# A gated expert layer on one core: the first pass's residual moved into the carried sums, and its results stored piece by piece

## The chip, the cores and the metric

The kernel runs on one core of one Trainium2 chip. The metric is the device time of one execution in microseconds (us), the median of several runs. The core has five engines that run side by side and meet at semaphores: PE (TensorE, matmuls; its weight loads are shown as PEld), DVE (VectorE), ACT (ScalarE), POOL (GpSimd) and SP (SyncE, which here issues nearly all DMAs).

## The reference

For eight batches of 512 rows and width 256, with nine "experts" (eight gated ones and a shared one) of inner width 1024:

```python
g = jnp.einsum('bsd,edf->ebsf', h, Wg)
u = jnp.einsum('bsd,edf->ebsf', h, Wu)
expert_outs = jnp.einsum('ebsf,efd->ebsd', jax.nn.silu(g) * u, Wd)
expert_output = jnp.einsum('be,ebsd->bsd', gating_probs, expert_outs)
shared = jnp.einsum('bsf,fd->bsd', jax.nn.silu(h @ Sg) * (h @ Su), Sd)
sg = shared_gate_prob[:, :, None]
return (1.0 - sg) * expert_output + sg * shared      # added to x
```

The result is `x` plus this. The `x +` is the residual that the change is about. All is in float32.

## The kernel before, in words

**Passes and units.** The eight batches are done in two passes (`h` = 0 and 1) of four. A pass goes through the nine experts, each in two groups of 512 inner columns, so it has 18 units and the kernel 36 (`u.n` = 0 to 35). A unit multiplies four blocks of weight columns (index i) with four batches (index j). To save products, blocks and batches are combined in pairs in the manner of fast matrix multiplication: `CI` holds the four numbers 0, 1, -1, 2, and `PAIRS` the six pairs.

**The hub basis.** Each batch is held transposed, in two halves of 128 features. `xhub[h, i][:, 1]` is the second half, X1. `xhub[h, i][:, 0]` is X0 - c X1, with c = `CI[i]`. Results come in the same basis: `acc["b", i]` is the first half of the result, `acc["B", i]` the second half plus c times the first; when a pass closes, c times the first is taken off.

**G steps and D steps.** `gate_up` makes the gate and up products of a unit in 52 G steps: 16 hub steps (`P_step`, `Q_step` and the first `R1_step`s), then six per pair (`R1_step`, two `R_step`s, twice). `down` makes the down products in 26 D steps: three for each pair, then `p0` to `p3` and `q0` to `q3`. PE does them in an order that is written out by hand, two G and one D in turn (`"GGD"`). The `down` of a unit starts at G step 22 of that unit and ends at G step 22 of the next one, so its eleven last steps (p0, q0, pair 5, q1, p1, q2, p2, q3, p3) lie in the first 11 D steps of the next unit.

**Carried banks.** D products go to two PSUM banks in turn (`po0`, `po1`). A "p" step is `carried`: ACT copies the running sum `acc["b", i]` into the bank (L578, the seed), PE adds its product (L579), ACT copies the bank back to SBUF (L587). A "q" step is `single`: PE writes the bank (L595) and DVE adds it to `acc["B", i]` (L566). The bank is free for the next product but one when that is done. The sums S of four pairs are carried like p.

**Who orders what.** Within `manual_schedule` the order on PE and POOL follows the program (and on ACT in unit 0). The order on DVE, SP, and on ACT from unit 1 on is laid out at build time by a planner that works with estimated durations. Each engine then runs its list in order, so an instruction that waits holds up all that stand behind it.

**Forms.** In unit 0 the pair forms of x are made on the chip: `x_difference` (DVE L288, ACT L290), `x_sums` (DVE L302 and POOL L303), `w_difference` (POOL L384) and `w_sums` (ACT L394, POOL L396 and L397). `store_forms` writes the x forms to DRAM. In later units SP loads them again: `v` by L292, `b` (two buffers) by L309. `prepare(1)` makes those of the second pass, in parts, during units 2 to 17. POOL also adds up the inner results for the p and q steps (`add_sum`, L540).

**The end of the first pass.** Unit 17 closes the pass; its last D steps lie in unit 18. `turn_back`, called at D steps 6, 10, 11, 13, 15, 18, 20 and 23 of unit 18, turns a result half with DVE (L669), adds x (L670), and after the second half of a batch stores four pieces of 128 KB (L673). x itself was loaded by `load_back` (L659) in four pieces per batch: two batches in unit 17, two more when buffers come free in unit 18. These tiles come from `iopool`, which has two buffers.

**The end of the second pass** has its own steps (`end_step`, `tail`, `store_rows`); its stores wait in a list, `end_stores`, of which one is issued per G step.

Of the kernel before, what the change touches and what calls it, by code (L numbers as in the profile page):

```python
# [16 lines left out]
def kernel(  # L17
# [95 lines left out]
    def make_coef():  # L113
# [4 lines left out]
            gp.tensor_tensor(coef[:, e, :], gt[:, :, e], rest, ALU.mult)  # L118
        gp.tensor_copy(coef[:, E, :], sgt)

    scratch = {}
    back = {}
    xhub = {}
    xdram = {}

# [424 lines left out]
    def down(u, acc):  # L550

        def tile_of(key):
            acc[key] = apool.tile(
                [P, S], F32, tag=f"acc{key[0]}{key[1]}", name=f"acc{key[0]}{key[1]}_{u.h}"
            )
            return acc[key]

        def put(key, bank, s):

            if key not in acc:  # L560
                if s == 1.0:
                    nc.scalar.copy(tile_of(key), bank)
                else:
                    nc.scalar.mul(tile_of(key), bank, s)
            elif s == 1.0:
                ve.tensor_add(acc[key], bank, acc[key])  # L566
            elif s == -1.0:
                ve.tensor_sub(acc[key], acc[key], bank)
            else:
                ve.scalar_tensor_tensor(acc[key], bank, s, acc[key], ALU.mult, ALU.add)  # L570

        def seeded(key, w, b):

            po, k = new_po(f"{key[0]}{key[1]}_{u.name}")
            full = key in acc and not turned[k]
            turned[k] = False
            if full:
                nc.scalar.copy(po, acc[key])  # L578
            nc.tensor.matmul(  # L579
                po, w, b, start=not full, stop=True, skip_group_check=full  # L580
            )
            return po, full

        def carried(key, w, b):
            po, full = seeded(key, w, b)
            if full:
                nc.scalar.copy(acc[key], po)  # L587
            else:
                put(key, po, 1.0)
            return po if full else acc[key]  # L590

        def single(key, w, b):
            po, k = new_po(f"{key[0]}{key[1]}_{u.name}")
            turned[k] = False
            nc.tensor.matmul(po, w, b, start=True, stop=True)  # L595
            return po, k

        def pair(p):
            i, j = PAIRS[p]
            d = CI[i] - CI[j]  # L600
            A, k = single(("r", p), u.Wd[p][i], u.h_[i, j])
            put(("B", j), A, 1.0)
            held[k] = True
            yield
            args = u.Wd[p][j], u.h_[j, i]
            if p in OWN and not closes(u):
                carried(("S", p), *args)
            else:
                if p in OWN:
                    o, full = seeded(("S", p), *args)  # L610
                    if not full:
                        ve.tensor_add(o, o, acc["S", p])
                else:
                    o, _ = single(("s", p), *args)
                put(("B", i), o, -1.0)
                put(("V", p), o, -1.0)
            yield
            nc.tensor.matmul(  # L618
                A, u.Ud[p], u.X[p], start=False, stop=True, skip_group_check=True
            )  # L620
            if closes(u):
                ve.tensor_add(A, A, acc["V", p])
                put(("b", i), A, 1.0 / d)
                put(("b", j), A, -1.0 / d)
            else:
                put(("V", p), A, 1.0)
            held[k] = False
            po_next[0] = 1 - k
            yield

        done = {}
        for what in (0, 1, 2, 3, 4, "p0", "q0", 5, "q1", "p1", "q2", "p2", "q3", "p3"):
            if isinstance(what, int):
                yield from pair(what)
                continue
            i = int(what[1])
            if what[0] == "p":
                flush_sums(u, "rows", i)
                done[what] = carried(("b", i), u.raw_d[:, i, 0:P], u.rows[i])
            else:  # L640
                flush_sums(u, "cols", i)
                po, _ = single(("q", i), u.ad[i], u.cols[i])
                put(("B", i), po, 1.0)
                done[what] = po
            if closes(u) and f"p{i}" in done and f"q{i}" in done:
                if CI[i] != 0.0:
                    put(("B", i), done[f"p{i}"], -CI[i])
                for r in (0, 1):
                    ends[u.h, i, r] = acc["bB"[r], i]
            yield  # L650

    BACK = [(0, 1), (0, 0), (2, 1), (2, 0), (1, 1), (1, 0), (3, 1), (3, 0)]

    def load_back(h, i):

        if (h, i) not in back:
            xr = iopool.tile([P, S // 32, 2, 32], F32, tag="io", name=f"xr{h}_{i}")
            for q in range(4):
                nc.sync.dma_start(xr[ts(q, 32)], squares(x, NI * h + i, q))  # L659
            back[h, i] = xr  # L660
        return back[h, i]

    def turn_back(h, i, r):

        b = NI * h + i
        block = ends.pop((h, i, r))
        xr = load_back(h, i)
        t = zpool.tile([P, S], F32, tag="z", name=f"to{b}_{r}")
        ve.transpose(t, block)  # L669
        ve.tensor_add(xr[:, :, r], t.rearrange("p (c d) -> p c d", d=32), xr[:, :, r])  # L670
        if (i, 1 - r) not in BACK[BACK.index((i, r)):]:
            for q in range(4):
                nc.sync.dma_start(squares(out, b, q), xr[ts(q, 32)])  # L673
            if i in (0, 2):
                load_back(h, i + 1)

    last_rows = {}
    tails = {}
    ended = {}
    end_rows = {}  # L680
    end_stores = []

    def end_step(kind, i):

        b = NI * (NH - 1) + i
        if kind == "turn":
            t = iopool.tile([P, 2, S], F32, tag="io", name=f"end{i}")
            for r in range(2):
                ve.transpose(t[:, r], ends.pop((NH - 1, i, r)))
            ended[i] = t  # L690
        elif kind == "store":
            to = end_rows[i] = dram.tile([S, D], F32, tag=f"end{i}", name=f"endrows{i}")
            at = to.rearrange("(c r t) d -> r t c d", r=32, t=NT)
            for r in range(2):
                for q in range(4):
                    end_stores.append((
                        at[:, :, :, ts(4 * r + q, 32)],
                        ended[i][ts(q, 32), r].rearrange("r (t c d) -> r t c d", t=NT, d=32),
                    ))
        elif kind == "x":  # L700
            last_rows[i] = load_rows(xpool, "x", b)
        elif kind == "load":
            at = end_rows[i].rearrange("(p t) d -> p t d", t=NT)
            end_rows[i] = []
            for c in range(2):
                t = sumpool.tile([P, 2, D], F32, tag="sum", name=f"endin{i}_{c}")
                nc.sync.dma_start(t, at[:, 2 * c : 2 * c + 2])
                end_rows[i].append(t)
        else:
            for xr, t in zip(last_rows[i], end_rows[i]):  # L710
                gp.tensor_tensor(xr, xr, t, ALU.add)
# [28 lines left out]
    def gate_up(u, nxt):  # L740
# [5 lines left out]
        def sums(p):  # L746
            x_sums(u, p)
            w_sums(u, p)
# [35 lines left out]
        for p in range(len(PAIRS)):  # L784
# [13 lines left out]
            for m in range(2):  # L798
                if not last:
                    R1_step(u, p + 1, m)  # L800
                    if m == 0 and u.n == 0 and p and p + 1 < len(PAIRS):
                        sums(p + 1)
                elif nxt is not None:
                    P_step(nxt, 0, m)
                yield
                for r in range(2):
                    R_step(u, p, m, r)
                    if m == 1 and r == 1:
                        h_sums(u, p)
                        if u.n == 0 and p + 2 < len(PAIRS):  # L810
                            seed(u, p + 2)
                        if p + 2 < len(PAIRS) and u.n:
                            sums(p + 2)
                    yield

# [16 lines left out]
        34: (("add", 1),), 37: (("load", 2),), 40: (("add", 2),), 44: (("load", 3),),  # L832
        47: (("add", 3),),
    }

    TAKE = 22

# [27 lines left out]
    for u in units:  # L865
# [6 lines left out]
        for what in FIRST if u.n == 0 else LAST if nxt is None else ORDER:  # L872
            if what == "G":
# [5 lines left out]
                    behind = down(u, acc) if nxt is not None else iter(())  # L879
                if final and nxt is not None and nG in (18, 21, 24, 27):  # L880
                    load_x(u.h + 1, (nG - 18) // 3)
                if final and nxt is not None and nG in (30, 36):
                    load_back(u.h, (nG - 30) // 3)
                if nxt is None:
                    for what_, i in END_STEPS.get(nG, ()):
                        end_step(what_, i)
                    if end_stores:
                        nc.sync.dma_start(*end_stores.pop(0))
                if nG > TAKE and nG % 2 == 0 and u.sums:
                    add_sum(u)  # L890
                for _ in range(2 if u.n and units[u.n - 1].opens else 1):
# [67 lines left out]
```

## Time and profile before

| what | us |
|---|---|
| median of 3 runs (lowest 2446.30, highest 2447.63) | 2446.37 |
| the profiled execution | 2446.47 |
| its span, first to last instruction | 2444.7 |
| PE busy in the span | 2431.5 |
| POOL busy | 2080.0 |
| DVE busy | 1928.9 |
| ACT busy | 1239.4 |

The granted clock of TensorE has a mean of 0.999. Lines of the profile name the engine, the line of the kernel (L513), the operation, and the tiles as out<-in. Lines of the timeline begin with the start and the length in us; "x2" means that two records were put together, and a bracket at the end tells how long the engine stood idle before and what released it. One float32 product of 128x128 by 128x512 is two records on PE. DMA issues are shown at the queue that issues them, SPq.

### The profile page before, as it was taken

The numbers are of one execution on the slowest core, as the hardware profiler recorded it, in microseconds if no ns is written. First come the engines' busy times: TensorE is split into PE (matmuls) and PEld (weight loads), VectorE is DVE, ScalarE is ACT, GpSimd is POOL, SyncE is SP. The second block draws the span as 40 slices with busy tenths as digits, with TensorE's granted clock in tenths as the row PEclk, the third lists the DMA queues.
The fourth block names the chain that finished last, engine by engine and source line by source line (L and its number), as shares of the span: only waits on it lengthen the run. The fifth ranks groups of instructions, "written<-read, shape, count | busy, mean of one in ns | idle before, by whom it ended". The sixth has DMA issues, their size and how long they took to land.

```text
span 2444.7 us, 22778 instructions
## 1 busy us (share of the span) xinstructions
PE 2431.5 (99%) x5736; PEld 1085.1 (44%) x5736; DVE 1928.9 (79%) x2870; ACT 1239.4 (51%) x2294; POOL 2080.0 (85%) x2313
## 2 busy tenths in 40 slices
PE   9999999999999999999999999999999999999999
PEld 4444444444444444444444444444444444444446
DVE  7778878777777877787987777777777777777795
ACT  5555554554555555555445555555555555555542
POOL 8988888898988989898878888888888888888872
PEclk9999999999999999999999999999999999999999
DMA  4333343343433333344353233323333333233245
GB/s 158 101 105 111 104 112 112 103 134 102 126 110 97 105 111 97 106 129 125 112 118 120 85 95 91 91 81 99 99 104 103 95 97 92 88 91 92 86 117 149
DMA packets 237841, 260.02 MB, mean 106 GB/s; under 512 B 80656, under 2 KB 173072, under 8 KB 237712
## 3 DMA queue, kind: packets, MB, share of 16 engines
q1 hardware_dynamic: 236880, 258.27, 35.9%
q8 instruction: 48, 0.79, 0.1%
q14 instruction: 81, 0.66, 0.1%
q10 hardware_dynamic: 832, 0.30, 0.0%
HBM read 240.69 MB, written 17.83 MB: 106 GB/s over the span
## 4 chain that ended last, share of the span: by engine, by line
PE 96%; POOL 1%; DVE 1%; DMA 1%; issue 0%; ACT 0%; SPq 0%; ACTq 0%; DVEq 0%; POOLq 0%
PE c L513 30%; PE c L503 15%; PE c L481 10%; PE c L458 10%; PE r L595 7%; PE r L618 7%; PE S L579 5%; PE b L579 5%; PE q L595 5%; PE s L595 2%; PE tail L720 1%; DMA sgt<-ondB_sharedgateprob_dram 0%; POOL wd L429 0%; POOL wb L396 0%; DVE h L449 0%
## 5 line engine op out<-in xcount | busy, mean ns | idle before, releaser
L513 PE MATMUL c<-b,wb 128*128 128x512 f32 x1728 | 848.1, 593 | 2.6 <-DMA b<-xs 1.9
L444 ACT ACTIVATE sg<-c 128x512 f32<-128x512 f32 x576 | 343.8, 597 | 595.0 <-DVE c L518 343.7
L449 DVE SCALAR_TENSOR_TENSOR h<-sg,coef,c 128x512 f32<-128x512 f32 x576 | 427.8, 743 | 235.6 <-PE c L513 128.3
L513 PEld LDWEIGHTS c<-b,wb 128*128 128x128 f32 x1728 | 328.3, 190 | 412.9 <-issue 390.0
L503 PE MATMUL c<-v,u 128*128 128x512 f32 x864 | 441.5, 593 | 1.9 <-ACT c L498 1.4
L540 POOL TENSOR_TENSOR rows<-rows,h 128x512 f32<-128x512 f32 x280 | 369.0, 1318 | 0.0
L508 DVE TENSOR_TENSOR c<-D,c 128x512 f32<-128x512 f32 x432 | 298.7, 692 | 81.1 <-ACT sg L444 61.4
L540 POOL TENSOR_TENSOR cols<-cols,h 128x512 f32<-128x512 f32 x280 | 357.7, 1277 | 0.0
L518 DVE TENSOR_TENSOR c<-c,D 128x512 f32<-128x512 f32 x432 | 298.6, 691 | 22.3 <-PE c L513 22.1
L396 POOL TENSOR_TENSOR wb<-u,wb 128x256 f32<-128x256 f32 x108 | 79.2, 733 | 237.3 <-ACT wb L394 237.3
L458 PE MATMUL c<-x,w 128*128 128x512 f32 x572 | 274.5, 592 | 0.0
L503 PEld LDWEIGHTS c<-v,u 128*128 128x128 f32 x864 | 163.0, 189 | 210.0 <-issue 163.9
L595 PE MATMUL r<-h,wd 128*128 128x512 f32 x420 | 215.4, 594 | 0.0
L618 PE MATMUL r<-X,ud 128*128 128x512 f32 x420 | 214.5, 592 | 0.0
L529 DVE TENSOR_TENSOR X<-h,h 128x512 f32<-128x512 f32 x210 | 206.1, 982 | 6.8
L481 PE MATMUL c<-x,at 128*128 128x512 f32 x432 | 209.4, 593 | 1.2 <-DVE P L474 0.7
L491 ACT COPY D<-c 128x512 f32<-128x512 f32 x284 | 165.8, 584 | 83.8 <-DVE h L449 83.8
L540 POOL TENSOR_TENSOR rows<-h,h 128x512 f32<-128x512 f32 x140 | 195.4, 1396 | 0.0
L540 POOL TENSOR_TENSOR cols<-h,h 128x512 f32<-128x512 f32 x140 | 181.0, 1293 | 0.0
L464 ACT COPY P<-c 128x512 f32<-128x512 f32 x216 | 126.6, 587 | 106.9 <-PE c L458 102.3
L458 PEld LDWEIGHTS c<-x,w 128*128 128x128 f32 x572 | 108.5, 190 | 135.9 <-issue 111.9
L578 ACT COPY S<-accS 128x512 f32<-128x512 f32 x132 | 77.9, 590 | 149.8 <-DVE accV L566 140.7
(108 smaller groups left out, 3472.5 us busy)
## 6 DMA issues: line engine op xcount, KB each, us to landing
b<-xs SPq DMA_DIRECT2D x210, 512.0 KB, 3.6
v<-xs SPq DMA_DIRECT2D x210, 256.0 KB, 2.6
wd<-in_L_cond_Wd_dram SPq DMA_DIRECT2D x32, 512.0 KB, 4.9
w<-in_L_cond_Wg_dram SPq DMA_DIRECT2D x127, 128.0 KB, 3.5
w<-in_L_cond_Wu_dram SPq DMA_DIRECT2D x127, 128.0 KB, 3.6
f<-xd SPq DMA_DIRECT2D x12, 512.0 KB, 3.6
xs<-f SPq DMA_DIRECT2D x18, 256.0 KB, 3.0
xin<-in_x_dram SPq DMA_DIRECT2D x16, 256.0 KB, 4.1
```

The lines of the kernel that those rows point to most:

```text
L444: nc.scalar.activation(s, bank, AF.Silu)
L449: ve.scalar_tensor_tensor(t, u.sg[i, j], coef[:, u.e, b : b + 1], bank, ALU.mult, ALU.mult)
L458: nc.tensor.matmul(bank, u.raw[i][:, m, 0], xhub[u.h, i][:, 0], start=True, stop=True)
L481: nc.tensor.matmul(bank, u.at[i][:, m], xhub[u.h, i][:, 1], start=False, stop=True, skip_group_check=True,)
L503: nc.tensor.matmul(bank, u.U[p][:, m], u.V[p], start=False, stop=True, skip_group_check=True)
L508: ve.tensor_sub(other, u.Ds[j, m], bank)
L513: nc.tensor.matmul(bank, u.W[p][:, r, m], u.VB[p][:, r], start=False, stop=True, skip_group_check=True,)
L518: ve.tensor_add(bank, bank, u.Ds[j, m])
L540: gp.tensor_tensor(sums[n], u.h_[n, n] if first else sums[n], u.h_[at], ALU.add)
L579: nc.tensor.matmul(po, w, b, start=not full, stop=True, skip_group_check=full)
L595: nc.tensor.matmul(po, w, b, start=True, stop=True)
L618: nc.tensor.matmul(A, u.Ud[p], u.X[p], start=False, stop=True, skip_group_check=True)
```

## The change

- The residual of the first pass is no longer loaded and added at the end. It is added in 14 of the units 3 to 16, one term in each: where a p or q step of that unit is due, its bank is seeded from the running sum and copied out by DVE with `acc = xhub * s + po` (`carried_with`). The terms per batch i are X0 - c X1 plus c times X1 for the b sum, and (1 + c c) X1 plus c (X0 - c X1) for the B sum; terms with factor 0 are left out. For q this puts a seed copy ahead of the product.
- `turn_back` only transposes, straight into the strided store tile; `load_back` and its calls are gone. The four store pieces of a batch go into a list, `outgoing`, of which one is issued per G step in any unit. The end of the second pass uses the same list.
- In unit 0, `sums(p + 2)` is called after the last `R_step` of pair p, as in the other units, and no longer after the `R1_step` that opens the next pair.
- A helper, `issue_after`, is defined and not called.

```diff
-            if what[0] == "p":
+            extra = carry_on.get(u.n)
+            if extra is not None and extra[0] == what:
+                flush_sums(u, "rows" if what[0] == "p" else "cols", i)
+                if what[0] == "p":
+                    key, w, b = ("b", i), u.raw_d[:, i, 0:P], u.rows[i]
+                else:
+                    key, w, b = ("B", i), u.ad[i], u.cols[i]
+                carried_with(key, w, b, *extra[1:])
+            elif what[0] == "p":
...
+        def carried_with(key, w, b, half, s):
+            po, full = seeded(key, w, b)
+            assert full
+            ve.scalar_tensor_tensor(
+                acc[key], xhub[u.h, key[1]][:, half], s, po, ALU.mult, ALU.add
+            )
...
+    for i in range(NI):
+        c = CI[i]
+        for what, half, s in (("p", 0, 1.0), ("q", 1, 1.0 + c * c), ("p", 1, c), ("q", 0, c)):
+            if s != 0.0:
+                carry_on[3 + len(carry_on)] = f"{what}{i}", half, s
...
     def turn_back(h, i, r):
 
-        b = NI * h + i
-        block = ends.pop((h, i, r))
-        xr = load_back(h, i)
-        t = zpool.tile([P, S], F32, tag="z", name=f"to{b}_{r}")
-        ve.transpose(t, block)
-        ve.tensor_add(xr[:, :, r], t.rearrange("p (c d) -> p c d", d=32), xr[:, :, r])
+        if i not in backs:
+            backs[i] = iopool.tile([P, S // 32, 2, 32], F32, tag="io", name=f"to{h}_{i}")
+        t = backs[i]
+        ve.transpose(t[:, :, r], ends.pop((h, i, r)).rearrange("p (c d) -> p c d", d=32))
         if (i, 1 - r) not in BACK[BACK.index((i, r)):]:
             for q in range(4):
-                nc.sync.dma_start(squares(out, b, q), xr[ts(q, 32)])
-            if i in (0, 2):
-                load_back(h, i + 1)
+                outgoing.append((squares(out, NI * h + i, q), t[ts(q, 32)]))
...
-                    if m == 0 and u.n == 0 and p and p + 1 < len(PAIRS):
-                        sums(p + 1)
...
-                        if p + 2 < len(PAIRS) and u.n:
+                        if p + 2 < len(PAIRS):
                             sums(p + 2)
...
-                if final and nxt is not None and nG in (30, 36):
-                    load_back(u.h, (nG - 30) // 3)
...
-                    if end_stores:
-                        nc.sync.dma_start(*end_stores.pop(0))
+                if outgoing:
+                    nc.sync.dma_start(*outgoing.pop(0))
```

More of the change, by code (lines that the diff above doesn't have):

```diff
@@ L119, in make_coef, with issue_after @@
         gp.tensor_copy(coef[:, E, :], sgt)
+    def issue_after(later, *first):
+        for at in first:
+            tc.add_manual_dep(
+                later.ins,
+                at.ins.name,
+                mybir.DependencyInfo(
+                    mybir.DependencyClass.NoSync, mybir.DependencyReason.DATA
+                ),
+                reason="issue order",
+            )
     scratch = {}
-    back = {}
+    backs = {}
+    outgoing = []
+    carry_on = {}
     xhub = {}
@@ L590, in carried @@
             return po if full else acc[key]
+        def carried_with(key, w, b, half, s):
[3 more added lines that the diff above has]
+                acc[key], xhub[u.h, key[1]][:, half], s, po, ALU.mult, ALU.add
+            )
         def single(key, w, b):
@@ L652 @@
     BACK = [(0, 1), (0, 0), (2, 1), (2, 0), (1, 1), (1, 0), (3, 1), (3, 0)]
[L654 to L661, printed above, removed]
-    def turn_back(h, i, r):
-        b = NI * h + i
-        block = ends.pop((h, i, r))
-        xr = load_back(h, i)
-        t = zpool.tile([P, S], F32, tag="z", name=f"to{b}_{r}")
-        ve.transpose(t, block)
-        ve.tensor_add(xr[:, :, r], t.rearrange("p (c d) -> p c d", d=32), xr[:, :, r])
+    def turn_back(h, i, r):
+        if i not in backs:
+            backs[i] = iopool.tile([P, S // 32, 2, 32], F32, tag="io", name=f"to{h}_{i}")
+        t = backs[i]
+        ve.transpose(t[:, :, r], ends.pop((h, i, r)).rearrange("p (c d) -> p c d", d=32))
         if (i, 1 - r) not in BACK[BACK.index((i, r)):]:
             for q in range(4):
-                nc.sync.dma_start(squares(out, b, q), xr[ts(q, 32)])
-            if i in (0, 2):
-                load_back(h, i + 1)
+                outgoing.append((squares(out, NI * h + i, q), t[ts(q, 32)]))
     last_rows = {}
@@ L680 @@
     end_rows = {}
-    end_stores = []
     def end_step(kind, i):
@@ L695, in end_step @@
                 for q in range(4):
-                    end_stores.append((
+                    outgoing.append((
                         at[:, :, :, ts(4 * r + q, 32)],
```

## The prediction

> **What bounds the kernel now.** First the page's busy table, then its chain of waits.
>
> ```profile
> PE 2431.5 (99%) x5736; PEld 1085.1 (44%) x5736; DVE 1928.9 (79%) x2870; ACT 1239.4 (51%) x2294; POOL 2080.0 (85%) x2313
> PE 96%; POOL 1%; DVE 1%; DMA 1%; issue 0%; ACT 0%; SPq 0%; ACTq 0%; DVEq 0%; POOLq 0%
> ```
>
> PE is busy for 99% and carries 96% of the chain. The change removes and adds no matmul. A gain can only come from the few places where PE stands still, a loss only from new ones. So I read the timeline of PE alone. A product is two records of 0.43 us, 0.86 us in all; a unit has 52 G and 26 D steps, 78 x 0.858 = 66.95 us. Any larger distance between starts is lost. Units 1 to 16 and 19 to 34 show almost nothing. Four places remain after the loading: unit 0, the closing units 17 and 35, and unit 18, which opens the second pass.
>
> ```profile
> 1258.89 1.02 PE L618 MATMUL r<-X,ud 128*128 128x512 f32 x2
> 1259.97 1.10 PE L503 MATMUL c<-v,u 128*128 128x512 f32 x2
> 1262.98 1.79 PE L513 MATMUL c<-b,wb 128*128 128x512 f32 x2 [1.91 <-DMA b<-xs]
> 1264.56 1.91 PE L595 MATMUL r<-h,wd 128*128 128x512 f32 x2
> 1266.27 1.22 PE L513 MATMUL c<-b,wb 128*128 128x512 f32 x2
> ```
>
> Here, in unit 18, PE waits for the load of `b` for pair 3. The next products take 1.6 to 1.7 us instead of 0.86: the clock has fallen. The window 1260 to 1268 has 0.79 of the clock; all others around it have 1.00. SP's timeline tells why the load was late:
>
> ```profile
> 1244.30 0.63 SPq L309 DMA_DIRECT2D b<-xs  x1
> 1252.05 0.57 SPq L673 DMA_DIRECT2D out_dram<-xr  x1
> 1252.81 3.00 SPq L659 DMA_DIRECT2D xr<-in_x_dram  x4
> 1255.86 2.53 SPq L673 DMA_DIRECT2D out_dram<-xr  x3
> 1258.49 0.62 SPq L309 DMA_DIRECT2D b<-xs  x1
> ```
>
> The buffer for that `b` was free when pair 1's last product ended, about 1250.5. But SP stood at a store of a turned result until DVE had added the residual (L670, 1251.38 to 1252.03), then issued eight residual transfers at some 0.65 us each. The load went out 8 us late. DVE has no idle time from 1227 to 1263 in its timeline, so what it does there delays something.
>
> In unit 0 it is POOL that runs without a gap (8.00 of 8.00 us in 40 to 48), and the sums of a pair come late:
>
> ```profile
> 39.32 1.20 DVE L288 TENSOR_TENSOR v<-x,x 128x512 f32<-128x512 f32 x1 [2.61 <-POOL b L303]
> 45.44 1.13 PE L503 MATMUL c<-v,u 128*128 128x512 f32 x2 [1.35 <-ACT c L498]
> 67.24 1.12 PE L513 MATMUL c<-b,wb 128*128 128x512 f32 x2 [0.64 <-POOL wb L396]
> ```
>
> **The change, part by part.**
>
> *Unit 18.* Removed: 16 loads of x (L659), 16 x 0.64 us of SP's time, of which eight lie ahead of late loads of `b`; and eight DVE adds (L670, median 0.70 us, once 1.57). The eight transposes stay, with the target now strided. No row has a strided transpose; L670, with strided output, is no dearer (0.70) than the contiguous L566 (0.68), so I take 0.70; a doubling would cost eight times 0.7 us of DVE, less than the adds give back. The stores are now in SP's queue one per G step, between the loads, and wait for a transpose only. Queued behind a store are v, b and the weights. For i = 2 the pieces go at G26 to G29 and `b` for pair 3 at G27. The last transpose of i = 2 ended at 1250.86 with three L670s ahead of it; without them about 1248. `b` can then leave at about 1251 and, at the 4.4 us that this load took, land by 1255.5, five us before it is needed.
>
> What PE gets back, by distances between starts in its timeline: the wait itself 1260.48 to 1262.98, less 0.43: 2.07; the slow products until 1267.32, 4.34 us for six records that need 2.57: 1.77; the L503 at 1251.95 (0.70) and its neighbour at 1259.97 (0.29), both behind the full DVE; the L579 at 1237.46 and the L503 after it (0.33), behind the add of 1234.19. Sum 5.2. The 0.42 at 1233.7 comes before most adds and stays.
>
> The clock part is weighed against the Trainium skill ("TensorE: Matmul & The Clock Gate", section "What's actually happening"): the gate falls to half after an idle window of about 3.4 us. By that rule a pause of 2.1 us would cost only itself, and this item 2.1 instead of 3.8, the sum 3.5. The row shows two products at about twice their time after the pause, so I take the row.
>
> Against it: the transposes for i = 1 and 3 need the buffer of i = 0 and 2, so DVE can stand until those stores land (2.8 us median). DVE has the removed adds as cover; without cover I allow up to 2 us, and count 0.3. Net gain 4.9, bounds 2 and 5.6.
>
> *Units 3 to 16, whose D steps run in the next unit.* One term each, 14 in all. In seven (p) the ACT copy L587 (0.586) becomes a DVE scalar_tensor_tensor. Its nearest row is L449, the same operation on one SBUF and one PSUM operand, 0.743. In the other seven (q) the DVE add L566 (0.684) becomes that operation, +0.06, and ACT gets a seed copy (L578, 0.590) ahead of the product. DVE grows by 7 x 0.743 + 7 x 0.06 = 5.6 us over 14 units. The skill speaks against this ("Perfetto Trace Analysis", section "Optimizing Scalar/DVE Operations"): work should move from a saturated DVE to Scalar, and p goes the other way. Taken at its word, as if DVE were on the path, it costs 5.6 us. But DVE is busy 53.4 of 68 us in these units and 26.3 of the 34 us (606 to 640) where these steps lie in one unit. I take nothing for the DVE time.
>
> The waits are what can cost. Behind p's operation waits the next seed into the same bank:
>
> ```profile
> 629.13 0.61 ACT L578 COPY b<-accb 128x512 f32<-128x512 f32 x1
> 632.13 1.02 PE L579 MATMUL b<-rows,wd 128*128 128x512 f32 x2
> 627.34 0.68 DVE L566 TENSOR_TENSOR accB<-q,accB 128x512 f32<-128x512 f32 x1
> 629.55 1.02 PE L595 MATMUL q<-cols,ad 128*128 128x512 f32 x2
> ```
>
> The seed ends 2.4 us before its product; over all steady units these margins are 2.2 to 2.9. A DVE operation 0.16 us longer than the copy, begun up to 1.5 us later because of DVE's queue, fits. A q seed adds a link: bank drained, copied, product. q1 and q3 find their bank drained over 2.6 us ahead, q0 3.4. Only q2 is tight: q1's bank is drained at 628.02, the copy ends at 628.7 at best and 629.8 behind two other copies, the product starts at 629.55. I count 0.2 us for each of the two units with q2: cost 0.4. From below: no unit has a PE wait here to remove, so no gain. From above: a seed queued behind one other waiting ACT operation, about 1 us in half of the seven q units, 4 us.
>
> *Unit 0.* `sums(p+2)` goes one G step earlier in POOL's and ACT's order. No operation is added. It is moved past `differences`, whose POOL subtract takes 0.72, past one L540 (1.27) where there is one, past ACT's L290 (0.63), and past `store_forms`, so SP can store that form earlier. What comes later instead is the pair's U (used 10 us on) and one L540, whose h buffers have a wait elsewhere (DVE L449 on POOL, 81.7 us in total). PE's losses from the rows above: 0.32 at 41.27 (late wb of pair 2, L397 ends 41.10), 1.62 at 45.44, 0.90 at 67.24. The first goes if POOL is 0.7 earlier. The second goes through L288, which waits for POOL L303, so 0.72 of it goes. The third I halve, as L396 stood after a subtract of the next unit. Sum 0.32 + 0.72 + 0.45 = 1.5; bounds -1.5 (h buffers later by one L540) and 2.8.
>
> Units 17 and 35 lose 2.1 us each on the seeds of S; the diff leaves these alone. The renamed list of end stores has the same order. `issue_after` is called nowhere.
>
> **The sum.** -4.9 - 1.5 + 0.4 = -6.0. The profiled execution took 2446.47 us (span 2444.7 and 1.77 around it), 0.10 above the median. So 2440.4 for the median.
>
> **The rivals.**
>
> *A, half is given back: 2443.6.* The transposes wait for store buffers or SP still stands at a store, so unit 18 returns only 2.8; unit 0 nothing. For it: DVE is full until 1263, and whatever is late there reaches PE. Against: SP loses its eight longest-standing issues. Chance 0.24.
>
> *B, the new link decides: 2452.6.* Each q product waits at its seed, and each p bank leaves late. With 0.9 us at each of 14 places the cost is 12.6 us against gains of 4.9 and 1.5, 6.2 us slower. It decides from 0.46 us per unit (6.4 / 14). For it: ACT and DVE work in order, and ACT often stands (`sg` on `c`, 343.7 us in total); a seed behind such a wait inherits it. Against: margins above 2 us in all but q2. Chance 0.13.
>
> *C, the residual changes nothing in unit 18 because the pieces hold up loads as before, and the order of unit 0 gets worse: 2447.* Chance 0.05.
>
> **How the numbers follow.** My forecast has 0.58, of which 2437.5 to 2442.5 is its own range. About 0.2%, 4.9 us, is what a measurement of this kernel can tell from no change. Faster than 2441.5: most of the forecast and the better end of A, 0.58. Slower than 2451.3: B, and C with a unit 0 at its worst, 0.14. Between: 0.28. The range 2437.5 to 2448.5 takes in A and C and leaves out B.
>
> **What would show it.** Right: no L659 and L670; in unit 18 a `b` load less than 2 us after its buffer is free, no PE wait on `b`, a clock of 1.00 in every window; distances of 0.86 in units 3 to 17 but for q2; the PE wait at 45 us shorter. Wrong: PE waits at L579 for ACT L578 in units 4 to 17 (B), or DVE waits for `out` stores in unit 18 (A).

## The result, and the profile after

| what | before, us | after, us |
|---|---|---|
| median of 18 runs each, on one chip | 2446.45 | 2442.16 |
| lowest and highest | 2445.49 to 2448.2 | 2440.25 to 2443.91 |
| the profiled execution | 2446.47 | 2443.3 |
| its span | 2444.7 | 2441.5 |

The ratio is 0.998 with a 95% interval of 0.9974 to 0.9986: the changed kernel is 4.3 us faster, between 3.4 and 6.4. No change is excluded. The line at 0.2% (4.9 us) that the prediction drew lies inside the interval, so on which side of it the gain falls is not settled. The profiled execution of after lies 1.1 us above its median.

The lines of the changed kernel have moved: L503 is now L517, L513 is L527, L579 is L593, L595 is L616, L618 is L639, L449 is L463, and further up L288 is L302, L302 is L316, L303 is L317, L309 is L323, L384 is L398, L540 is L554. The busy table and the chain of waits, as before:

```profile
PE 2430.0 (100%) x5736; PEld 1084.7 (44%) x5736; DVE 1923.6 (79%) x2869; ACT 1239.4 (51%) x2294; POOL 2076.4 (85%) x2313
PE 96%; POOL 1%; DMA 1%; DVE 1%; issue 0%; ACT 0%; SPq 0%; ACTq 0%; DVEq 0%; POOLq 0%
```

The matmuls are the same 5736. To see where the time went I use one measure throughout, **PE's lost time**: the distances between the starts of successive PE records, each less 0.4292 us (the 66.95 us of a unit by its 156 records), summed over a stretch. It counts waits and halved-clock products alike.

| stretch | before | after |
|---|---|---|
| unit 0 (30 to 72 us) | 3.32 | 4.66 |
| unit 9 (600 to 700) | 0.01 | 1.56 |
| close of unit 17 (1170 to 1222) | 2.15 | 2.13 |
| unit 18 (1222 to 1300) | 5.59 | 0.34 |
| closing end (after 2300) | 2.49 | 2.47 |

Unit 18 gave back 5.25; units 0 and 9 lost 2.9 more in these two executions. (The two are 3.2 apart. The 0.8 that is missing lies ahead of the table: the changed kernel's PE reached unit 0 some 0.8 earlier.) First unit 18, in PE's timeline of the changed kernel:

```profile
1259.89 1.02 PE L639 MATMUL r<-X,ud 128*128 128x512 f32 x2
1260.75 1.02 PE L517 MATMUL c<-v,u 128*128 128x512 f32 x2
1261.61 1.02 PE L527 MATMUL c<-b,wb 128*128 128x512 f32 x2
1262.47 1.02 PE L616 MATMUL r<-h,wd 128*128 128x512 f32 x2
```

Every distance is 0.86. The product on `b` that stood 1.91 us waits for nothing, and the two at half the clock are gone. SP's timeline:

```profile
1245.00 0.61 SPq L323 DMA_DIRECT2D b<-xs  x1
...
1252.36 0.33 SPq L323 DMA_DIRECT2D b<-xs  x1
1253.21 0.58 SPq L905 DMA_DIRECT2D out_dram<-to  x1
1260.09 0.32 SPq L323 DMA_DIRECT2D b<-xs  x1
```

The load of `b` that left at 1258.49 now leaves at 1252.36. In the windows of this stretch DVE has idle time again:

```profile
1250.00:1260.00 10.00, 10.00 (x25) 4.48 (x24) 7.75 (x11) 6.41 (x12) 6.41 (x7) 1.00 0.36 94
1260.00:1268.00 8.00, 8.00 (x20) 3.50 (x19) 7.07 (x12) 3.53 (x7) 4.87 (x6) 1.00 0.75 166
```

The columns after the length of the window are the busy times of PE, PEld, DVE, ACT and POOL, the granted clock, the DMA share and GB/s. The clock is 1.00 in both, where before it had 0.79 in the second.

Unit 0 is not better. Its timelines (PE, then DVE) of the changed kernel:

```profile
45.20 1.81 PE L517 MATMUL c<-v,u 128*128 128x512 f32 x2 [2.04 <-ACT c L512]
46.80 1.92 PE L593 MATMUL S<-h,wd 128*128 128x512 f32 x2
```

```profile
38.40 1.20 DVE L302 TENSOR_TENSOR v<-x,x 128x512 f32<-128x512 f32 x1 [2.49 <-POOL b L317]
42.09 1.77 DVE L316 TENSOR_TENSOR b<-v,x 128x512 f32<-128x512 f32 x1
43.79 0.73 DVE L463 SCALAR_TENSOR_TENSOR h<-sg,coef,c 128x512 f32<-128x512 f32 x1
```

The wait at 45 us has grown from 1.35 to 2.04, and now the clock falls behind it: products of 1.6 to 1.7 us, as before in unit 18. DVE's wait for POOL before `v` of pair 5 is still there (2.61, now 2.49). The same stretch in the kernel before, DVE, then POOL:

```profile
43.02 1.09 DVE L302 TENSOR_TENSOR b<-v,x 128x512 f32<-128x512 f32 x1
44.03 0.73 DVE L449 SCALAR_TENSOR_TENSOR h<-sg,coef,c 128x512 f32<-128x512 f32 x1
```

```profile
42.29 1.27 POOL L540 TENSOR_TENSOR cols<-h,h 128x512 f32<-128x512 f32 x1
```

The terms are the new operation at L609:

```profile
L609 DVE SCALAR_TENSOR_TENSOR accb<-x,b x7: 676/678/680, 278.5 to 1109.4; 128x512 f32<-128x512 f32 x7
L609 DVE SCALAR_TENSOR_TENSOR accB<-x,B x7: 677/689/689, 348.3 to 1173.5; 128x512 f32<-128x512 f32 x7
```

0.68 to 0.69 us, at the price of the add that it replaces in the q steps. PE waits for no seed of a q step. The strided transposes (L688) have a median of 0.693 us.

### The profile page after: what moved, and what is told of

It reads as the page before. It is cut to its first block, busy times and chain, and to the rows that moved or that the text cites. A ratio compares the mean times of both kernels' runs of the same rounds, so it can differ in the third digit from the quotient of the medians.

```text
span 2441.5 us, 22760 instructions
## 1 busy us (share of the span) xinstructions
PE 2430.0 (100%) x5736; PEld 1084.7 (44%) x5736; DVE 1923.6 (79%) x2869; ACT 1239.4 (51%) x2294; POOL 2076.4 (85%) x2313
## 4 chain that ended last, share of the span: by engine, by line
PE 96%; POOL 1%; DMA 1%; DVE 1%; issue 0%; ACT 0%; SPq 0%; ACTq 0%; DVEq 0%; POOLq 0%
PE c L527 29%; PE c L517 15%; PE c L495 10%; PE c L472 10%; PE r L616 7%; PE r L639 7%; PE b L593 5%; PE S L593 5%; PE q L616 5%; PE s L616 2%; PE tail L735 1%; DMA b<-xs 1%; PE B L593 0%; DMA sgt<-ondB_sharedgateprob_dram 0%; POOL wd L443 0%
## 5 line engine op out<-in xcount | busy, mean ns | idle before, releaser
L527 PE MATMUL c<-b,wb 128*128 128x512 f32 x1728 | 847.5, 592 | 1.1 <-DMA b<-xs 1.1
L463 DVE SCALAR_TENSOR_TENSOR h<-sg,coef,c 128x512 f32<-128x512 f32 x576 | 427.3, 742 | 242.2 <-PE c L527 139.5
L527 PEld LDWEIGHTS c<-b,wb 128*128 128x128 f32 x1728 | 328.3, 190 | 411.3 <-issue 386.8
L517 PE MATMUL c<-v,u 128*128 128x512 f32 x864 | 441.8, 593 | 2.0 <-ACT c L512 2.0
L554 POOL TENSOR_TENSOR rows<-rows,h 128x512 f32<-128x512 f32 x280 | 368.8, 1317 | 1.4 <-DVE h L463 1.4
L554 POOL TENSOR_TENSOR cols<-cols,h 128x512 f32<-128x512 f32 x280 | 358.2, 1279 | 0.0
L517 PEld LDWEIGHTS c<-v,u 128*128 128x128 f32 x864 | 163.4, 190 | 209.1 <-issue 163.6
L616 PE MATMUL r<-h,wd 128*128 128x512 f32 x420 | 214.5, 592 | 0.0
L639 PE MATMUL r<-X,ud 128*128 128x512 f32 x420 | 214.5, 592 | 0.0
L554 POOL TENSOR_TENSOR rows<-h,h 128x512 f32<-128x512 f32 x140 | 194.0, 1386 | 0.0
L554 POOL TENSOR_TENSOR cols<-h,h 128x512 f32<-128x512 f32 x140 | 180.2, 1287 | 0.0
```

The costliest lines, as they stand in the source:

```text
L463: ve.scalar_tensor_tensor(t, u.sg[i, j], coef[:, u.e, b : b + 1], bank, ALU.mult, ALU.mult)
L517: nc.tensor.matmul(bank, u.U[p][:, m], u.V[p], start=False, stop=True, skip_group_check=True)
L527: nc.tensor.matmul(bank, u.W[p][:, r, m], u.VB[p][:, r], start=False, stop=True, skip_group_check=True,)
L554: gp.tensor_tensor(sums[n], u.h_[n, n] if first else sums[n], u.h_[at], ALU.add)
L639: nc.tensor.matmul(A, u.Ud[p], u.X[p], start=False, stop=True, skip_group_check=True)
```

## The experiments

Two theories of unit 18 stood against each other. **The queue**: the sixteen loads of x on SP delay the loads of `b`. **The adds**: DVE's eight additions keep it full, so that what stands behind them, the stores on SP among it, is late. For the terms, the question was whether they cost anything; for unit 0, why nothing came. The groups ran on different chips, so each names the median of the kernel before on its own chip, and a ratio is always to that.

### One part of the change undone

**after_again** is the changed kernel once more, the reference of this group (before: 2445.97).

> The changed kernel once more, to stand beside the others on the same chip. If the waits on b in unit 9 (1.0 and 0.4 us at 647 and 656 us in the profile) are an accident of that execution, they are gone or smaller here, and the time is 2442 again. If the new seeds or the order cause them, they are there again with the same length. The wait in unit 0 near 43 us: 2.2 us with the clock halved after it if the new order fixes it; another length if it hangs on the phase in which DVE and POOL meet.

Measured: 2441.91 us, ratio 0.9984 (0.9975 to 0.9993). Unit 18 loses 0.34, unit 0 2.91, unit 9 0.34: what after lost in units 0 and 9 is not fixed to the kernel.

**sums_back** puts the `sums` call of unit 0 back:

```diff
                     R1_step(u, p + 1, m)
+                    if m == 0 and u.n == 0 and p and p + 1 < len(PAIRS):
+                        sums(p + 1)
...
-                        if p + 2 < len(PAIRS):
+                        if p + 2 < len(PAIRS) and u.n:
                             sums(p + 2)
```

> The changed kernel with the sums of unit 0 called where they were before. The prediction's step: the new place gains 1.5 us, so this is 1.5 slower than the changed kernel, about 2443.7. The theory after the profile: the new place costs 0.8 to 2 us (PE lost 4.3 us between 39 and 49 us, 1.9 before, while 0.9 at 66 us went), so this is 2440.5 to 2441.5, with the 0.9 at 66 us back.

2442.18 us, ratio 0.9986 (0.9977 to 0.9994): 0.3 from the changed kernel, which is nothing, and neither of the two times expected. Unit 0 loses 3.87. The move that the prediction counted at 1.5 us brings nothing here.

**at_once** stores the four pieces together:

```diff
-                outgoing.append((squares(out, NI * h + i, q), t[ts(q, 32)]))
+                nc.sync.dma_start(squares(out, NI * h + i, q), t[ts(q, 32)])
```

> The changed kernel with the four store pieces of a batch issued at once where the second half is turned, not one per G step. If the gain in unit 18 is that no residual is loaded or added, nothing changes: PE loses under 1 us between 1230 and 1290 us, time within 0.7 of the changed kernel. If it is the spacing of the stores that lets the loads of b through, the wait on b in unit 18 returns (2 to 4 us slower).

2442.14 us, ratio 0.9985 (0.9976 to 0.9994), unit 18 loses 0.34. To store one piece per G step is worth nothing once the adds and loads are gone.

**all_terms** adds a term at every p and q step of units 3 to 16, 112 in place of 14:

```diff
-            extra = carry_on.get(u.n)
+            extra = (what, i % 2, 1.0) if u.n in carry_on else None
```

> All eight p and q steps of units 3 to 16 go through the new path, 112 in place of 14; x is added many more times than it should be, so the output is another sum. If a term costs nothing (the margins above 2 us hold it), the time stays within 1 us of the changed kernel; the prediction's 0.2 us at each q2 would be 14 x 0.2 = 2.8 us more against 0.4; rival B with 0.46 us or more per term would be 98 x 0.46 = 45 us slower. A wait, if any, is expected at the q2 product on ACT's seed.

2443.92 us, ratio 0.9992 (0.9983 to 1.0): 2.0 above the changed kernel for 98 terms more, where at most 1 was expected. In its PE timeline there is one new loss, 0.058 us at the seeded product of q2 in each of the 14 units, 0.8 in all. The rest of the 2.0 lies in units 0 and 9 in the one execution traced, and I can't give it to the terms. So q2 was rightly named as the tight place, and its price is 0.06, not 0.2.

### One part of the change alone

These start from the kernel before (2446.21 on this chip). The planner lays out DVE's and SP's order anew for each, so a run shows a part together with the order that it brings. The runs also differ by up to 2 us in when unit 18 begins, so I count `b`'s departure from the start of the DVE operation that completes the store ahead of it: in the kernel before, from the add at 1251.38 to the load at 1258.49, 7.1 us.

**loads_no_adds** leaves the adds out and keeps all loads of x; the residual of the first pass is therefore missing from its output:

```diff
-        t = zpool.tile([P, S], F32, tag="z", name=f"to{b}_{r}")
-        ve.transpose(t, block)
-        ve.tensor_add(xr[:, :, r], t.rearrange("p (c d) -> p c d", d=32), xr[:, :, r])
+        ve.transpose(xr[:, :, r], block.rearrange("p (c d) -> p c d", d=32))
```

> The kernel before with the eight adds of x (L670) left out: the first pass's output lacks x, but x is still loaded and the stores are issued four at a time. If SP's eight loads are what made b of pair 3 late in unit 18, PE still waits on b there (1 to 2 us, with the clock halved after it) and the gain over the kernel before is under 2 us. If it is DVE's adds, for which the stores waited at SP's head, b goes out by 1255 us, PE waits under 0.3 us, and the gain is 4 to 5 us.

2442.53 us, ratio 0.9984 (0.9975 to 0.9994), 3.7 below the kernel before. Unit 18 loses 0.33. Four loads of x stand right in the place that the prediction blamed, in SP's timeline:

```profile
1251.57 0.33 SPq L309 DMA_DIRECT2D b<-xs  x1
1251.94 0.43 SPq L292 DMA_DIRECT2D v<-xs  x1
1252.55 4.63 SPq L659 DMA_DIRECT2D xr<-in_x_dram  x4
1259.29 0.33 SPq L309 DMA_DIRECT2D b<-xs  x1
```

but in the planner's new order `b` is ahead of them, and no store holds the queue until DVE has added. So taking out the adds is enough for the whole gain; what these loads would cost if they stood ahead of `b` is not shown.

**adds_no_loads** is the counterpart: no loads of x, and the transposed block is added to itself in place of x:

```diff
-            for q in range(4):
-                nc.sync.dma_start(xr[ts(q, 32)], squares(x, NI * h + i, q))
...
-        ve.tensor_add(xr[:, :, r], t.rearrange("p (c d) -> p c d", d=32), xr[:, :, r])
+        tt = t.rearrange("p (c d) -> p c d", d=32)
+        ve.tensor_add(xr[:, :, r], tt, tt)
```

> The kernel before with the 16 loads of x (L659) left out and the adds kept (each turned half is added to itself, so the first pass's output is another sum). If the loads are the cause, the wait on b in unit 18 is gone (3.8 us) and the small losses behind a full DVE stay (0.3 at 1237, 0.7 at 1251, 0.3 at 1259): gain 3.5 to 4.5 us. If the adds are the cause, the store still stands at SP's head until about 1251 us and some of the wait on b stays: gain under 2 us.

2447.65 us, ratio 1.0005 (0.9995 to 1.0014): the whole gain is gone. Unit 18 loses 5.74. SP's timeline, then DVE's, then PE's:

```profile
1254.22 2.76 SPq L672 DMA_DIRECT2D out_dram<-xr  x4
1257.08 0.63 SPq L309 DMA_DIRECT2D b<-xs  x1
```

```profile
1259.53 2.36 DVE L669 TENSOR_TENSOR xr<-to 128x512 f32<-128x512 f32 x2
...
1263.01 0.73 DVE L449 SCALAR_TENSOR_TENSOR h<-sg,coef,c 128x512 f32<-128x512 f32 x1
```

```profile
1264.44 1.10 PE L503 MATMUL c<-v,u 128*128 128x512 f32 x2 [2.37 <-POOL cols L540]
```

The store still waits at the head of SP's queue for the add (it issues at 1254.22, when the L669 of 1253.55 is done). But without the four loads behind it `b` leaves 3.5 us after that add begins, in place of 7.1, and PE does not wait for it. The wait that the prediction read was in part made by the loads, then; without them it has another name and a like length. Two adds that take 2.36 us together stand ahead of the h product (L449), and PE waits 2.37 us at the L503 that starts 0.70 after h is done. The profile puts that wait down to POOL's L540. That DVE's adds are behind it is read from the timeline, where DVE has no gap from 1253 to 1263.7.

**pieces_only** stores one piece per G step, nothing else:

```diff
-                nc.sync.dma_start(squares(out, b, q), xr[ts(q, 32)])
+                end_stores.append((squares(out, b, q), xr[ts(q, 32)]))
...
-                    if end_stores:
-                        nc.sync.dma_start(*end_stores.pop(0))
+                if end_stores:
+                    nc.sync.dma_start(*end_stores.pop(0))
```

> The kernel before with only the stores of the first pass put into the list, one per G step; x is loaded and added as before. The theory (spacing is worth nothing, the adds and loads are the cause): the wait on b in unit 18 stays or grows, time within 1 us of before. The rival (spacing lets b through): a gain of 3 to 4 us. Unit 9 has the same instructions as in the kernel before, so any wait on b there beyond 0.1 us is not the change's.

2446.34 us, ratio 0.9998 (0.9989 to 1.0008): no gain, as expected. That the wait on `b` would stay was a miss. Behind the loads of x only one store piece, not three, is still ahead of `b`; it leaves 5.2 us after the add began, and PE's wait for it fell from 1.91 to 0.43. Unit 18 loses only 2.17, but 1.84 comes after 1300 us, where PE waits for an inner sum of POOL:

```profile
1261.64 1.10 PE L513 MATMUL c<-b,wb 128*128 128x512 f32 x2 [0.43 <-DMA b<-xs]
1305.51 1.13 PE L595 MATMUL q<-cols,ad 128*128 128x512 f32 x2 [1.57 <-POOL cols L540]
```

That this is the same lateness, passed on from DVE, is not shown by the trace. What speaks for it is the sum. From 1222 to 1400 us, and without the 1.7 to 1.8 us of products at half the clock where there are any, the kernels that keep the adds lose 3.8 (before), 4.1 (adds_no_loads), 4.0 (this one) and 4.3 (sums_only, below), wherever the wait stands; those without adds lose 0.3.

**sums_only** moves the `sums` call of unit 0, nothing else:

```diff
-                    if m == 0 and u.n == 0 and p and p + 1 < len(PAIRS):
-                        sums(p + 1)
...
-                        if p + 2 < len(PAIRS) and u.n:
+                        if p + 2 < len(PAIRS):
                             sums(p + 2)
```

> The kernel before with only the sums of unit 0 moved. The prediction's step: 1.5 us faster than before. What the profiles show so far of the new place: PE waits 1.8 to 2.2 us near 43 us, sometimes with the clock halved for 1.7 us, and 0.9 at 66 us is gone; with the sums back the losses of unit 0 from 30 us were 3.9 against 2.9, 3.9, 4.1 and 4.7 with them moved. So 0.5 slower to 0.5 faster than before, and unit 18 as before with its 3.8.

2446.6 us, ratio 1.0001 (0.9992 to 1.0011): nothing, as in sums_back. It also gives a second look at the old unit 18, which this edit doesn't touch (PE's timeline):

```profile
1261.83 1.10 PE L503 MATMUL c<-v,u 128*128 128x512 f32 x2
1264.26 1.10 PE L513 MATMUL c<-b,wb 128*128 128x512 f32 x2 [1.33 <-DMA b<-xs]
1265.19 1.02 PE L595 MATMUL r<-h,wd 128*128 128x512 f32 x2
```

Here `b` came 0.6 sooner, the clock did not fall, and the stretch lost 3.86 where the execution that the prediction was made from lost 5.59.

### What blocks unit 0

DVE stands 2.5 us before `v` of pair 5 because the `v` buffers are in use until POOL's L317 has read one. **v5_io** gives that one `v` a tile from the pool of the store buffers, which are unused in unit 0; the rest is the changed kernel (its lines from here on are 3 higher):

```diff
-        v = vpool.tile([P, S], F32, tag="v", name=f"v{u.name}_{p}")
+        if u.n == 0 and p == 5:
+            v = iopool.tile([P, 2, S], F32, tag="io", name=f"v{u.name}_{p}")[:, 0]
+        else:
+            v = vpool.tile([P, S], F32, tag="v", name=f"v{u.name}_{p}")
```

> The changed kernel with one edit: in unit 0 the difference v of pair 5 gets a tile of iopool (idle in unit 0) in place of the third v buffer, which POOL's sum for pair 2 still reads. Theory: in unit 0 DVE stands 2.5 us at that subtract (L302 there), and what is late behind it (the R1_step subtracts, the h products, then ACT's seed) makes the wait near 43 us, 1.8 to 2.2 us with the clock sometimes halved after it; so the wait falls under 0.7 us, the clock stays whole, unit 0 loses under 2 us from 30 to 70 us (2.9 to 4.7 now), and the time is 1.5 to 2.5 us below the changed kernel. Rival: POOL, which runs without a gap there, is the bound; DVE then waits for POOL elsewhere and the time does not move.

2440.46 us against 2445.89, ratio 0.9978 (0.9969 to 0.9987): the best median of all. It is 5.4 below the kernel before, after_again 4.1 on its chip; the intervals overlap. Unit 0 loses 1.44. PE's timeline has no wait left at 45 us:

```profile
44.24 1.12 PE L520 MATMUL c<-v,u 128*128 128x512 f32 x2
```

**v5_io_back** is v5_io with the `sums` call put back as in sums_back.

> The same edit with the sums of unit 0 back in their old place. If POOL's order is what matters now, the waits for POOL's wb (0.3 to 1.3 at 41 us, 0.9 at 66 us) stay and this is 1 to 2 us slower than the edit with the sums moved: the gain that the prediction gave to the move would come out once DVE's stand is gone. If not, the two are equal within 0.5 us.

2444.07 us, ratio 0.9993 (0.9984 to 1.0002), 3.6 above v5_io on the same chip. Unit 0 loses 3.75, most of it in one place of PE's timeline:

```profile
68.65 1.13 PE L530 MATMUL c<-b,wb 128*128 128x512 f32 x2 [2.30 <-POOL wb L413]
```

So the move of `sums` is worth more than it was counted for once DVE doesn't stand; neither of the two alone gains anything (the move: after_again beside sums_back, 2441.91 and 2442.18; the tile: v5_io_back beside sums_back, by their ratios 0.9993 and 0.9986).

**no_terms** is the changed kernel without any of the 14 terms, so the residual of the first pass is missing (`if s is None` in place of `if s != 0.0`).

> The changed kernel with none of the 14 terms: units 3 to 16 as in the kernel before, no x in the first pass's output, turn_back and the stores as changed. If the terms cost nothing, time and PE's losses are those of the changed kernel within 0.5 us; the prediction's cost of the terms was 0.4, rival B's at least 6.4 us.

2441.91 us against 2445.89, ratio 0.9983 (0.9974 to 0.9992); after_again has 0.9984, on another chip. The terms cost nothing that these runs can tell.

**v5_late** is v5_io with one more rule for the planner: `v` of pair 5 is to be issued behind the last subtract of `R1_step`, so that it doesn't delay the first products.

```diff
+            made = ve.tensor_sub(v, xhub[u.h, i][:, 0], xhub[u.h, j][:, 0])
+            if p == 5:
+                issue_after(made, u.r1)
...
+        u.r1 = ve.tensor_sub(other, u.Ds[j, m], bank)
```

> The changed kernel with v of pair 5 in the iopool tile and its DVE subtract kept behind the last R1_step subtract issued before it, by issue_after, so that the planner does not pull it ahead into the hub (where the first form of this edit lost 1.8 us before 30 us against 1.0). If both losses are DVE's order, the first 30 us lose 1.0 again, 30 to 70 us stays near 1.4, and the time is 2439 to 2440. If the subtract now comes late for ACT and pair 5, a wait appears at 58 to 67 us.

2441.3 us (2439.2 to 2443.2) against 2445.47, ratio 0.9982 (0.9973 to 0.9991). The 0.8 us that v5_io lost between 20 and 30 us (1.85 against 1.02) did come back in its trace, and unit 0 lost the same 1.44; the time shows no gain over v5_io. A miss: differences of this size drown in the spread of the runs.

## Why the prediction was right or wrong

**Unit 18, -4.9: right in size, in part right in cause.** The stretch gave back 5.25 in the two profiles, by the items named: the wait on `b`, the products at half the clock, the waits behind the full DVE. The halved-clock products went with the wait, as counted. No transpose waited for a store, for which 0.3 had been set aside. What the sum had wrong is where the wait came from. It was read as a late load: a store at the head of SP's queue, then "eight residual transfers" (four of them are loads of x, four the pieces of the store). That is how `b` came to be late; but taking the loads out (adds_no_loads) or spacing the stores (pieces_only) shortened its wait to nothing and to 0.43, and gained no time, for PE then waited elsewhere. Taking only the adds out gained all of it (loads_no_adds). So "removed: 16 x 0.64 us of SP's time" was worth nothing while the adds stood, and the adds, 7.4 us of DVE's time and mostly where it is full, were what paid, by DVE's own lateness and by the store that waits on them. How much each of these two ways is worth the runs don't separate.

**Unit 0, -1.5: wrong, about 0.** Three items were summed. The third, the `wb` wait at 67 us, went altogether (0.9, halved to 0.45 in the sum). The first, at 41 us, is 0.25 to 1.6 in the five profiles with the old order and at most 0.2 in the new. The second is where the step failed: "so 0.72 of it goes". The wait at 45 us did not fall but grew, from 1.52 of lost time in all five old-order profiles to 1.84 to 2.21 in all six new-order ones. The lines above show how, once the times are counted from the start of `v` of pair 5. (That it starts 0.92 earlier, 38.40 in place of 39.32, isn't the 0.72 foreseen: 0.79 of it is only that this execution's PE reached unit 0 earlier, as the same product shows that starts at 30.62 here and at 31.41 before.) PE's last record before the wait starts 4.17 after `v` in all five old-order profiles. It has just waited at 41 us for POOL, whose order `v` follows too, so when both come earlier the distance stays. What changed is `h`: 4.71 after `v` in the old order, 5.39 in the new, in every profile. Between the two lies DVE's sum of forms, 1.09 us before and 1.77 now. It starts 3.70 after `v` in both, but the moved call has left POOL's subtract (L398, 0.72) standing ahead of its inner sums, so the POOL operation that the sum meets began 0.73 before it then and begins 0.03 before it now. The 0.68 more goes into PE's wait: 1.52 + 0.68 = 2.20 in after and sums_only. In the other four PE no longer waits at 41 us, comes 0.36 later after `v`, and 1.84 is left. In four of the six profiles the clock also fell behind the pause (some 1.7 us more). Lost in unit 0: on average 4.2 in the old order, 3.9 in the new. The prediction had allowed for a loss here by POOL's L540; it did not look at what DVE's two-input add meets on POOL.

**The terms, +0.4: no cost.** The operation took 0.68, not 0.743 that was taken from L449, but the size didn't matter. The rule of the Trainium skill that spoke against moving work to DVE ("Perfetto Trace Analysis", section "Optimizing Scalar/DVE Operations"), at 5.6 us if DVE were on the path, did not decide: no_terms has a ratio of 0.9983, after_again with the terms 0.9984. In the stretch itself DVE stays busy for 26.2 of 34 us.

**The rivals.** B, the new link, is refuted: 14 terms cost nothing that shows, and 98 more some 2.0 us. At the 0.46 us per term from which B decides, those 98 would have cost 45. A came as near as the forecast (2443.6 and 2440.4, measured 2442.16), for the wrong reason: unit 18 returned all, not half, and no transpose waited for a store. Nor did C come about.

**The size, -6.0 against -4.3.** Without the terms and unit 0 the sum is 4.9. The rest is that one execution was taken for the kernel: the old unit 18 lost 5.59 in the execution that was read and 3.86 in sums_only, where its code is the same. Less the 0.34 of after that is 5.25 and 3.52, 4.4 in the middle, beside the measured 4.3. The 1.73 between them is the halved clock, of which the prediction counted 1.77 as sure; it comes and goes between executions of the same code. With two traces this is an estimate, no more.

**What the signs said.** No L659 and L670, no wait on `b` in unit 18, clock 1.00 there: as foreseen. The PE wait at 45 us is longer, not shorter. The distances of 0.86 in units 3 to 17 failed in one place, unit 9:

```profile
648.28 1.10 PE L527 MATMUL c<-b,wb 128*128 128x512 f32 x2 [0.85 <-DMA b<-xs]
```

The change isn't needed for this. sums_only, pieces_only, loads_no_adds and adds_no_loads have unit 9 as before and lose 0.57, 0.55, 1.11 and 1.33 there. The loss in that place lies anywhere between 0.01 and 2.16 in the fourteen profiles, and the one of before happened to show 0.01.

## What to carry to other kernels

The wait that a profile names may be only the last of several that one late engine makes. Here shortening the queue in front of `b` shortened the wait on `b`, twice, and gained no time; relieving the full DVE of its eight adds gained it all. So before a queue is shortened, ask what its head waits for, and what PE would wait for next. And a gain that is read from waits of less than a microsecond in one execution should be looked at in a second one, since such waits come and go between runs of the same code; a step moved ahead in one engine's order also changes what another engine meets there.

## What the runs showed of the hardware

**Two engines take turns at SBUF.** DVE's sum of two SBUF operands waits for the POOL operation that is running, then needs some 0.55 us. POOL's timeline of the changed kernel beside the L316 of 42.09 shown above:

```profile
42.06 1.26 POOL L554 TENSOR_TENSOR cols<-h,h 128x512 f32<-128x512 f32 x1
43.28 1.71 POOL L317 TENSOR_TENSOR b<-v,x 128x512 f32<-128x512 f32 x1
```

L316 begins 0.03 after L554 and ends 0.54 after L554 does: 1.23 of waiting, 0.54 of work. The POOL operation behind it takes 1.71 in place of 1.26. In the kernel before, POOL's operation ran from 42.29 to 43.56 and the sum from 43.02 to 44.11: 0.54 of waiting and 0.55 of work. The Trainium skill ("SBUF — State Buffer", section "Who interferes with whom") says that a DVE instruction with two SBUF inputs contends with a GpSimd instruction that reads SBUF, one with at most one such input does not; the trace agrees on both, since L609 with one operand in PSUM stays at 0.68 to 0.69 in all 14 places, in 12 of which POOL was at work.

**A pause of two microseconds can halve the clock, and needn't.** After an idle time of 1.91 (unit 18 before) and 2.04 (unit 0 after) the products ran at half the clock. After 1.33 (unit 18 in sums_only) they did not. A pause that cost 1.84 us in unit 0 left the clock alone in after_again and no_terms, and halved it in at_once and all_terms. The length alone doesn't tell, then; where the pause falls does. In each of the six falls before the last product the clock is halved for 3.41 us, and the fall comes a whole number of such stretches after the clock first rose (1256.1 us, 368 stretches, in before; 40.96 us, 12 stretches, in after). So I cut the time into this grid. Two slices of all_terms, then two of no_terms, with PE's busy time after the length:

```profile
43.34:46.75 3.41, 1.73 (x4) 0.51 (x4) 2.99 (x4) 1.98 (x5) 2.76 (x4) 1.00 0.22 89
46.75:50.16 3.41, 3.41 (x5) 1.33 (x5) 0.70 (x1) 2.80 (x6) 3.41 (x4) 0.50 0.62 226
```

```profile
43.27:46.68 3.41, 1.85 (x4) 0.78 (x5) 2.48 (x4) 2.49 (x6) 2.76 (x4) 1.00 0.36 148
46.68:50.10 3.42, 3.42 (x9) 1.51 (x9) 2.78 (x5) 2.18 (x5) 3.42 (x5) 1.00 0.49 162
```

In the fourteen profiles the clock fell after every slice in which PE stood for 1.67 us or more (six, 1.67 to 2.30), and after none with 1.56 or less. In after_again the same pause lies across two slices, 0.73 and 0.95, and the clock stays. So the 3.4 us of the page that the prediction cites agree as the length of the slice, but PE needn't stand for a whole one: here 1.67 us of it was enough. The prediction's choice of the row over the page held a second time, in unit 0: a pause of two microseconds may cost some 1.7 us more behind it, by the luck of where it falls.
